# Kept weight sums, a later place for two steps of level sums, and outputs behind the next group's products in a transformer block

## The chip, the cores and the metric

The kernel runs on one core of one Trainium2 chip. The metric is the device time of one execution in microseconds. In the profile, PE is TensorE's matmul, PEld its weight load, DVE is VectorE, ACT is ScalarE, POOL is GpSimd, and SP is SyncE, which here only issues DMAs. A name with a q (SPq, POOLq, ACTq) is that engine's instruction queue.

## The reference

The input x holds 32 sequences of 64 tokens with 1024 features, in fp32. A block of four layers is computed, with one residual around the first two and one around the last two:

```python
x = x + attn(cond(x, label))        # cond: x W^T + LoRA chosen by the sequence's label
x = x + ffn(cond2(x, language))     # both: x W^T + a top-2 mixture of 8 LoRA experts of rank 16
```

The attention has 32 heads of 32 features, 8 key and value heads, rotary embedding and a causal mask. Nothing non-linear stands between cond and the projections of q, k and v, nor between cond2's base and ffn's base.

## The kernel before

**Products.** Every large product is one of 2 x 2 blocks done with seven products instead of eight (Strassen's scheme in Winograd's form). `Group` (L236) is one such product: the steps p1 to p7 each multiply one factor of the weights with one of the columns (`mult`, L268, whose matmul is L270), into three PSUM banks x, y and z. p1 goes to x and is copied to SBUF by ACT (L291); p6 goes to y and is taken out by DVE with p1 added (L297, "u1"); p5 goes to z; p7 adds to y, and is taken out (L309, "u2"); `out11` takes z out; p2 adds to x; p3 adds to z and p4 to y, and both are taken out. A bank that is accumulated on or reused has to be taken out first, so DVE's place in these steps matters to PE. The weights' factors are four sums of a weight tile, made on POOL by `weight_sums` (L171; its four additions are L180, L182, L184 and L186). The columns' sums are made on DVE by `column_sums` (L189; L195, L197, L199, L201).

**Stages.** First the weights are merged, once: cond into the projections of q, k and v (cq and ckv, `multiply` at L722 and L755, into the DRAM tensor `cqkv`), and cond2 into ffn (cf, L852, into `cf7`). Then the tokens go in two halves (`hf`, L967). In each half: six `qk_pair` products (L1025; pairs 4, 0, 1, 2, 3, 5, of which 4 are k and 5 are v), the attention in eight units, the output projection (`o_pairs`), and the feed-forward part, in 14 `quarter` groups (L1490).

**cf's levels.** In the feed-forward part each of the seven products is itself one of 2 x 2 blocks, so `cf7` holds the weights of both levels. `levels` (L823) makes them on DVE while cf's groups are multiplied: `level_one` (L803) makes sums of cf's blocks, `level_two` (L813 to L816) the four sums of one factor, and SP stores four parts of it (L818). The table `after` of L854 tells behind which step of which group (`(2, "p7")` is group 2's p7) each of them is recorded; PE, DVE and SP keep this order, as it is recorded under `tc.manual_schedule`. DVE takes cf's banks out at L603 (all blocks but the first) and adds the identity at L606. Each of these writes into a block of the tile `cf`, which is shared by groups 0 and 2 and by groups 1 and 3. `levels(0, "p6")` and `levels(0, "p7")` read the block "12" of groups 0 and 1; p4 of group 2 overwrites it. `narrow` (L769) is a small product behind some groups. `wo_sums` (L781) loads a part of the output projection's weights, makes their sums on POOL and stores them (L787) for later; its tiles have one buffer each.

**The pairs.** `qk_pair` loads a pair's merged weights w with SP, makes their sums s with POOL, in both halves, and returns a `RankGroup`. Its tiles w and s have two buffers each, so that those of one pair come free when the pair before the last is done with them. Pair 5's sums are made in two parts: the first when the pair is made (L1273), the others behind p4 of pair 3 (L1281). In the second half pair 4 is recorded to be issued behind the last sum of the first half's feed-forward part (L1166).

**The feed-forward groups.** `Quarter` (L351) splits its steps in `begin` (p1, p6), `middle` (p5, p2, p7, out11; in the last group of a half p5, p7, p2, out11) and `end` (p4, p3). The loop at L1608 records the begin of one group, the end of the one before, and the middle:

```python
group = quarter(n, r)
group.begin()
...
if last is not None:
    finish(last)
...
group.middle((n, r) == (6, 1), behind)
```

`finish` (L1553) is the end and, for the two groups of n = 4 alone, the sums that give two blocks of output: POOL adds z to b (L1560), DVE makes the output (L1562), and ACT issues its store (L1565). `known` (L1509) adds further products on POOL (L1512). PE and POOL keep the recorded order there; DVE's order is a scheduler's.

**The beginning.** DVE clears a tile (L130) and PE multiplies it (L133), ahead of the first loads' landing.

Of the kernel before, what the change touches and what calls it, by code (L numbers as in the profile page):

```python
# [13 lines left out]
F32 = mybir.dt.float32  # L14
# [5 lines left out]
P = 128  # L20
# [55 lines left out]
def block_kernel(ctx: ExitStack, tc: tile.TileContext, a, out: bass.AP):  # L76
    nc = tc.nc
# [48 lines left out]
        )  # L126
    )

    idle = tmp("idle")
    nc.vector.memset(idle, 0.0)  # L130
    ps = ps_tile("idle")
    for n in (512,):
        nc.tensor.matmul(ps[:, :n], idle[:, :P], idle[:, :n], start=True, stop=True)  # L133
    bqkv, bo, bb = biases[:, 0:12], biases[:, 12 : 12 + KC], biases[:, 12 + KC :]

# [215 lines left out]
    class Quarter(Group):  # L351
# [11 lines left out]
            self.p6()  # L363

        def middle(self, last=False, behind=None):
            two = (self.p7, self.p2) if last else (self.p2, self.p7)
            self.p5()
            if behind is not None:
                behind()
            for step in (*two, self.out11):  # L370
                step()

        def end(self):
            self.p4()
# [137 lines left out]


    cf7 = scratch.tile([P, 7, 8, 2, 2, P], F32, tag="cf7", name="cf7")
    FACTORS = ("s1", "s2", "11", "21", "12", "22", "s3", "s4")
    b1q = const.tile([P, NQ], F32, tag="b1q", name="b1q")
    b1d = const.tile([P, 6, P], F32, tag="b1d", name="b1d")
# [8 lines left out]
    with tc.tile_pool(name="gen", bufs=1) as gen:  # L526
# [320 lines left out]
        def first_w(w):  # L847
# [14 lines left out]
                (1, "p3"): lambda w: levels(0, "p3"),  # L862
                (1, "p4"): lambda w: narrow(1, w),
                (2, "p6"): lambda w: (levels(0, "p4"), wo_sums(5)),
                (2, "p7"): lambda w: (levels(0, "p6"), wo_sums(6)),
                (2, "p2"): lambda w: levels(0, "p7"),
                (2, "p3"): lambda w: wo_sums(7),
                (2, "p4"): first_w,
                (3, "out11"): lambda w: levels(1, "out11"),
                (3, "p2"): lambda w: levels(1, "p2"),  # L870
# [96 lines left out]
    for hf in range(2):  # L967
# [57 lines left out]
        def qk_pair(g, z_bank=group_bank, sums=range(4)):  # L1025
            w = first_pass.pop(f"w{g}", None)
            if w is None:
                w = load_w(cqkv[:, :, g * WG : (g + 1) * WG], f"qk{hf}{g}")

            def out(r, c, ps, add):  # L1030
                oc = 2 * g + r
                raw = tmp(f"raw_{hf}_{oc}_{c}")
                bias = bqkv[:, oc : oc + 1]
                if add is None:
                    nc.scalar.activation(raw, ps, AF.Identity, bias=bias)
                else:
                    nc.vector.scalar_tensor_tensor(raw, ps, bias, add, ALU.add, ALU.add)
                if g == 5:
                    v_blocks[r, c] = raw
                else:  # L1040
                    rope(oc, c, raw)

            def rank(r, c, rows):
                b = b1d[rows, g, :] if (r, c) == (0, 1) else b1q[rows, (2 * g + r) * P : (2 * g + r + 1) * P]
                return b, low_half(c)[rows]

            s = weight_sums(w, f"qk{hf}{g}", None, sums)
            pair = RankGroup(f"qk{hf}{g}", w, s, xt, out, rank, z_bank)
            pair.w_and_s = w, s
            return pair  # L1050
# [203 lines left out]
        with tc.manual_schedule():  # L1254

            rotated()
            pair, held = qk_pair(2), None
            for u in range(2):
                g = pair
                g.p1()  # L1260
                g.p6()
                if u == 0:
                    g.p5()
                    masked(u)
                else:
                    masked(u)
                    g.p5()
                maxima(u)
                g.p7()
                g.p2()  # L1270
                normalised(u)
                if u == 1:
                    pair = qk_pair(5, sums=(0,))  # L1273
                g.together(held)
                if u == 0:
                    pair = qk_pair(3, ps_tile)
                held = g
                g.p4()
                if u == 1:
                    w, s = pair.w_and_s  # L1280
                    weight_sums(w, None, s, (1, 2, 3))  # L1281
                g.p3()


            g, ws = pair, {}
            g.p1()
            g.p5()
            ws[0] = turned(0, in_place_of(1, "ws0"))
            g.some((0, 0), (1, 1), held=held)
            held.out01()  # L1290
            g.p6()
            prepared(2)
            ws[1] = turned(1, in_place_of(2, "ws1"))
            rotated()
            normalised(2)
            g.p7()
            g.out11()
            prepared(3)
            g.p2()
            g.out(0, 0, g.x, None)  # L1300
            g.some((1, 0), (0, 1))
            wo0 = o_load(0, 0)
            ws[2] = turned(2, in_place_of(3, "ws2"))
            normalised(3)
            g.p4()
            prepared(4)
            g.p3()
            g.out01()
            v_turned(0)
            ws[3] = turned(3, in_place_of(4, "ws3"))  # L1310
            v_turned(1)
            normalised(4)
            masked(5)
            for u in range(4):
                banks = iter((group_bank, ps_tile if u % 2 else group_bank))
                values(u, ws[u], lambda name: next(banks)(name))
                if u == 1:
                    two = [in_place_of(j, f"sums_o{j}") for j in (1, 2)]
                    t0 = [t[:, 2 * i : 2 * i + 2] for t in two for i in range(2)]
                    o_sums(0, t0, 0, 2)  # L1320
            o_sums(0, t0, 2, 4)
            maxima(5)
            wo1 = o_load(0, 1)
            ot = Columns(o_columns(0), 512, 2, [[t[:, kc, :] for kc in range(2)] for t in t0])
            pairs = o_pairs(0, 0, wo0, ot, (group_bank, group_bank))
            pairs += o_pairs(0, 1, wo1, ot, (group_bank, group_bank))
            for u in range(4, 8):
                o = pairs[u - 4]
                ws = turned(u, in_place_of(3 + u % 2, f"ws{u}"))
                o.p1()  # L1330
                if u == 7:
                    t1 = [
                        [ep.tile([P, 512], F32, tag="e", name=f"sumo{hf}{j}{kc}") for kc in range(2)]
                        for j in range(4)
                    ]
                    o_sums(1, t1, 4, 7)
                sc = scores(u + 2) if u < 6 else None
                o.p6()
                if u < 7:
                    normalised(u + 1)  # L1340
                if u < 6:
                    masked(u + 2, sc, range(2))
                o.p5()
                o.p7()
                if u < 6:
                    masked(u + 2, sc, range(2, 4))
                o.out11()
                o.p2()
                if u < 6:
                    maxima(u + 2, range(2))  # L1350
                if u == 6:
                    wo0 = o_load(1, 0)
                values(u, ws)
                o.p4()
                if u < 6:
                    maxima(u + 2, range(2, 4))
                o.p3()
            o_sums(1, t1, 7, 8)
            ot = Columns(o_columns(1), 512, 2, t1)
            wo1 = o_load(1, 1)  # L1360
            pairs = o_pairs(1, 0, wo0, ot, (group_bank, ps_tile))
            pools.close()

            yp = scoped(f"sums_y{hf}", side="right")
            xt = columns(f"y{hf}", yp, x_half, 512)
            for p in range(2):
                for step in ("p1", "p6", "p5", "p7", "p2", "out11", "p4", "p3"):
                    for o in pairs:
                        getattr(o, step)()
                    if p == 1 and step in ("p5", "out11"):  # L1370
                        xt.make(("p5", "out11").index(step))
                pairs = o_pairs(1, 1, wo1, ot, (group_bank, ps_tile))
            attention.close()
# [176 lines left out]
            group.n_q = n, q  # L1550
            return group

        def finish(group):  # L1553
            group.end()
            n, q = group.n_q
            if SEVEN[n][0] == "p5":
                for m in range(2):
# [9 lines left out]
        with tc.manual_schedule(engines={mybir.EngineType.PE, mybir.EngineType.Pool}):  # L1567
# [40 lines left out]
            for n in range(7):  # L1608
# [10 lines left out]
                for r in range(2):  # L1619
# [5 lines left out]
                    if r == 0 and n < 6:  # L1625
                        differences_of[n + 1] = experts_difference(n + 1)
                    if last is not None:
                        finish(last)
                    behind = {(0, 0): next_logits, (0, 1): next_turned}.get((n, r))
                    group.middle((n, r) == (6, 1), behind)  # L1630
                    if (n, r) == (0, 1):
                        hw[1] = scaled("3", hf, [h[1, c] for c in range(2)], late["gs"])
                        through.update({"21": hw[1][0], "22": hw[1][1]})
                        nc.vector.tensor_sub(et[:, 1], hw[1][1], et[:, 0])
                        nc.vector.tensor_sub(hw[0][1], hw[1][1], hw[0][1])
                    if r == 0 and n < 6:
                        ts[n + 1] = inner_columns(n + 1)
                    last = group
            finish(last)
        pools.close()  # L1640


# [86 lines left out]
```

## Time and profile before

| | us |
|---|---|
| Median of 3 runs | 1195.55 |
| The three runs | 1189.01, 1195.59, 1195.55 |
| The profiled execution | 1194.38 |
| Its span, first to last instruction | 1192.6 |
| PE busy | 1176.1 |
| DVE, POOL, ACT busy | 707.1, 551.0, 163.8 |

The profile is of one execution. Its own time is 1.8 us longer than its span, and 1.2 us shorter than the median of the runs. Positions in time are given from the start of the span: the weights are merged until about 299 us, the first half of the tokens goes from there to about 740 us, and the second to the end. A matmul in fp32 shows as two instructions, and its end is modelled, so that a group of eight instructions of 512 columns is printed as 3.60 us while the next follows after 3.43. The granted clock of TensorE is 1 at full speed.

### The profile page before, as it was taken

How to read it: one execution, taken by the hardware profiler on the slowest of the kernel's cores; microseconds unless marked ns; L12 is line 12 of the kernel's file. 1: busy time of each engine (PE TensorE's matmuls, PEld its weight loads, DVE VectorE, ACT ScalarE, POOL GpSimd, SP SyncE). 2: the span in 40 equal slices, each digit the busy share in tenths (PEclk: the TensorE clock that was granted, in tenths of full speed). 3: DMA queues.
4: the chain of work that ended last, by engine and by line, in shares of the span. 5: the costliest groups of instructions: out<-in, count | busy, mean ns of one | idle time of the engine just before them, and what ended most of it. 6: DMA issues, size and time to landing. Idle time of an engine off the chain costs nothing.

```text
span 1192.6 us, 14868 instructions
## 1 busy us (share of the span) xinstructions
PE 1176.1 (99%) x5752; PEld 673.4 (56%) x5752; DVE 707.1 (59%) x1215; ACT 163.8 (14%) x314; POOL 551.0 (46%) x491
## 2 busy tenths in 40 slices
PE   9999999989999999999999999999999999999998
PEld 3444874545444446544458888444446544448887
DVE  3214162638555878874647664756788874657563
ACT  1100000000000115430011000100114530011000
POOL 1452355360343667662703654344677661801342
PEclk9999999999999999999999999999999999999999
DMA  9553644867311122022315668111121022203544
GB/s 318 169 212 127 265 147 142 276 210 253 92 35 36 36 72 71 2 71 71 103 32 164 185 184 259 36 39 35 37 70 50 24 71 71 93 16 102 154 144 139
DMA packets 120373, 137.60 MB, mean 115 GB/s; under 512 B 6768, under 2 KB 98928, under 8 KB 119024
## 3 DMA queue, kind: packets, MB, share of 16 engines
q1 hardware_dynamic: 105312, 111.65, 30.0%
q10 hardware_dynamic: 12304, 16.62, 4.0%
q0 software_dynamic: 2688, 8.39, 2.0%
q8 instruction: 45, 0.74, 0.3%
q14 instruction: 24, 0.20, 0.1%
HBM read 101.94 MB, written 34.71 MB: 115 GB/s over the span
## 4 chain that ended last, share of the span: by engine, by line
PE 93%; DVE 5%; issue 1%; DMA 1%; SPq 0%; ACT 0%
PE qk_y L270 10%; PE o_y L270 7%; PE qk_z L270 7%; PE qk_x L270 7%; PE f_y L270 6%; PE o_z L270 5%; PE o_x L270 5%; PE f_z L270 4%; PE f_x L270 4%; PE cq_y L270 4%; PE sc L1078 3%; PE cf_y L270 3%; PE cq_x L270 3%; PE pt L1137 2%; PE cq_z L270 2%; PE cf_z L270 2%
## 5 line engine op out<-in xcount | busy, mean ns | idle before, releaser
L1013 POOL TENSOR_TENSOR raw<-raw,consts 128x512 f32<-128x512 f32 x40 | 62.8, 1579 | 105.2 <-DVE t L1012 105.2
L270 PE MATMUL qk_y<-sum_x,s_qk 128*128 128x512 f32 x192 | 87.7, 597 | 2.3 <-DVE sum_x L197 2.1
L1111 POOL TENSOR_TENSOR e<-e,top 128x512 f32<-128x512 f32 x64 | 66.3, 1054 | 48.5 <-DVE top L1110 46.9
L270 PE MATMUL qk_x<-x,w_qk 128*128 128x512 f32 x192 | 86.8, 595 | 0.0
L270 PE MATMUL f_y<-s_f,w_f 128*128 128x256 f32 x336 | 82.8, 380 | 2.1 <-DVE f_u L309 2.1
L1129 POOL TENSOR_TENSOR e<-e,tot 128x512 f32<-128x512 f32 x64 | 64.8, 1045 | 28.7 <-DVE tot L1127 27.3
L270 PEld LDWEIGHTS f_y<-s_f,w_f 128*128 128x128 f32 x336 | 63.6, 190 | 11.9 <-DVE f_u L309 3.4
L270 PEld LDWEIGHTS qk_y<-sum_x,s_qk 128*128 128x128 f32 x192 | 35.6, 190 | 48.0 <-issue 40.7
L270 PEld LDWEIGHTS qk_x<-x,w_qk 128*128 128x128 f32 x192 | 36.1, 190 | 45.3 <-issue 45.0
L270 PE MATMUL o_x<-q,w_o 128*128 128x512 f32 x128 | 58.9, 592 | 0.0
L1248 POOL TENSOR_TENSOR x<-x,o_u 128x512 f32<-128x512 f32 x24 | 30.9, 1291 | 54.5 <-DVE o_u L1246 33.2
L1014 DVE TENSOR_TENSOR t<-t,consts 128x512 f32<-128x512 f32 x40 | 49.7, 1253 | 0.7
L1101 DVE TENSOR_TENSOR e<-sc,consts 128x512 f32<-128x512 f32 x64 | 41.2, 677 | 11.0 <-PE sc L1078 11.0
L1121 ACT ACTIVATE e<-e 128x512 f32<-128x512 f32 x64 | 37.9, 639 | 58.9 <-POOL e L1111 58.8
L1126 DVE TENSOR_REDUCE tot<-e 128x8 f32<-128x512 f32 x64 | 40.3, 666 | 7.4 <-ACT e L1121 7.3
L934 POOL COPY gatesr<-oh1r 128x1024 f32<-128x1024 f32 x4 | 4.1, 1037 | 86.8 <-DVE oh1r L932 86.8
L270 PE MATMUL qk_y<-sum_x,w_qk 128*128 128x512 f32 x96 | 44.2, 603 | 0.0
L270 PE MATMUL qk_z<-x,s_qk 128*128 128x512 f32 x96 | 43.4, 594 | 0.0
L270 PE MATMUL qk_z<-sum_x,s_qk 128*128 128x512 f32 x96 | 43.4, 594 | 0.0
L1110 DVE TENSOR_REDUCE top<-e 128x8 f32<-128x512 f32 x64 | 41.3, 679 | 0.8
L1023 DVE TENSOR_TENSOR q<-raw,t 128x512 f32<-128x512 f32 x32 | 38.5, 1204 | 2.5 <-POOL raw L1013 2.3
L1139 ACT COPY ws<-pt 128x512 f32<-128x512 f32 x64 | 33.4, 608 | 40.7 <-PE pt L1137 40.7
(382 smaller groups left out, 2363.9 us busy)
## 6 DMA issues: line engine op xcount, KB each, us to landing
w_f<-cf SPq DMA_DIRECT2D x28, 512.0 KB, 4.6
w_qk<-cqkv SPq DMA_DIRECT2D x12, 1024.0 KB, 5.5
w_f<-cf SPq DMA_DIRECT2D x28, 384.0 KB, 4.7
x<-in_xT SPq DMA_DIRECT2D x16, 512.0 KB, 6.4
w_o<-in_wo SPq DMA_DIRECT2D x16, 512.0 KB, 4.4
s_o<-wos SPq DMA_DIRECT2D x16, 512.0 KB, 6.3
outT<-o ACTq DMA_DIRECT2D x20, 256.0 KB, 4.2
cqkv<-cq ACTq DMA_DIRECT2D x16, 256.0 KB, 5.3
```

Of the source, the lines that this page charges most:

```text
L270: self.last = nc.tensor.matmul(ps, self.weights[left][:, kc, :], self.right(right, kc), start=first and kc == 0, stop=kc == self.h - 1, sk ...
L1013: nc.gpsimd.tensor_mul(rv, rv, c3)
L1014: nc.vector.tensor_mul(t2v, t2v, s3)
L1023: nc.vector.tensor_add(*unfinished.pop())
L1078: nc.tensor.matmul(sc[j][:, n * S : (n + 1) * S], q[rows, g, b, 2 * mp : 2 * mp + 2, :].rearrange("p m t -> p (m t)"), k[rows, g, b, :], s ...
L1101: nc.vector.tensor_add(per_key(e), per_key(sc[j]), mask.unsqueeze(1).to_broadcast([P, 8, S]))
L1110: nc.vector.tensor_reduce(top, ev, AX.X, ALU.max)
L1111: nc.gpsimd.tensor_sub(ev, ev, wide(top))
L1121: nc.scalar.activation(e, e, AF.Exp, scale=SCALE)
L1126: nc.vector.tensor_reduce(tot[:, i], es[i], AX.X, ALU.add)
L1129: nc.gpsimd.tensor_mul(es[i], es[i], wide(tot[:, i]))
L1139: nc.scalar.copy(ws, pt)
```

## The change

Four things are changed.

1. `qk_pair` makes the sums s in the first half only. It stores them in a new DRAM tensor `sqk` with a DMA of 1 MB issued by POOL (pair 5's after its second part). In the second half s is loaded from there, by SP, and for pair 4 by POOL.
2. In cf's table, `levels(0, "p6")` moves from behind p7 of group 2 to behind its out11, and `levels(0, "p7")` from behind its p2 to behind its p3, ahead of `wo_sums(7)`. `wo_sums(6)` stays behind p7, so that its load is now ahead of the stores of levels p6 on SP.
3. What `finish` did after the end of a group is now `sums_out`, recorded behind the next group's middle. In the last group of a half, p7 is now ahead of p5.
4. The first tile is cleared in 256 columns, and multiplied three times.

```diff
-    idle = tmp("idle")
+    idle = tmp("idle")[:, :256]
...
-    for n in (512,):
+    for n in (256, 256, 256):
         nc.tensor.matmul(ps[:, :n], idle[:, :P], idle[:, :n], start=True, stop=True)
...
         def middle(self, last=False, behind=None):
-            two = (self.p7, self.p2) if last else (self.p2, self.p7)
+            if last:
+                self.p7()
             self.p5()
             if behind is not None:
                 behind()
-            for step in (*two, self.out11):
-                step()
+            self.p2()
+            if not last:
+                self.p7()
+            self.out11()
...
+    sqk = scratch.tile([P, 6, 4, H, P], F32, tag="sqk", name="sqk")
...
                 (2, "p6"): lambda w: (levels(0, "p4"), wo_sums(5)),
-                (2, "p7"): lambda w: (levels(0, "p6"), wo_sums(6)),
-                (2, "p2"): lambda w: levels(0, "p7"),
-                (2, "p3"): lambda w: wo_sums(7),
+                (2, "p7"): lambda w: wo_sums(6),
+                (2, "out11"): lambda w: levels(0, "p6"),
+                (2, "p3"): lambda w: (levels(0, "p7"), wo_sums(7)),
...
-            s = weight_sums(w, f"qk{hf}{g}", None, sums)
+            if hf == 0:
+                s = weight_sums(w, f"qk{hf}{g}", None, sums)
+                if len(sums) == 4:
+                    nc.gpsimd.dma_start(sqk[:, g], s)
+            else:
+                s = wp.tile([P, 4, H, P], F32, tag="s", name=f"s_qk{hf}{g}")
+                (nc.gpsimd if g == 4 else nc.sync).dma_start(s, sqk[:, g])
...
-                if u == 1:
+                if (u, hf) == (1, 0):
                     w, s = pair.w_and_s
                     weight_sums(w, None, s, (1, 2, 3))
+                    nc.gpsimd.dma_start(sqk[:, 5], s)
...
-        def finish(group):
-            group.end()
+        def sums_out(group):
             n, q = group.n_q
             if SEVEN[n][0] == "p5":
...
                     if last is not None:
-                        finish(last)
+                        last.end()
                     behind = {(0, 0): next_logits, (0, 1): next_turned}.get((n, r))
                     group.middle((n, r) == (6, 1), behind)
+                    if last is not None:
+                        sums_out(last)
...
-            finish(last)
+            last.end()
```

## The prediction

> **What bounds the kernel now.** I read the page's busy shares first, then the waits of PE (TensorE matmul), then the timelines around each.
>
> ```profile
> PE 1176.1 (99%) x5752; PEld 673.4 (56%) x5752; DVE 707.1 (59%) x1215; ACT 163.8 (14%) x314; POOL 551.0 (46%) x491
> ```
>
> PE is busy 1176.1 of 1192.6 us, so no change that leaves its products alone can win more than about 16 us plus what its matmuls lose to a lower clock or to restarts. PE's waits (who waited for whom: total us, times, longest) are few:
>
> ```profile
> PE cf_z L270 <- DVE cf L603: 4.4, 1, 4.4
> PE f_y L270 <- DVE f_u L309: 2.1, 3, 0.9
> PE qk_y L270 <- DVE sum_x L197: 2.1, 4, 0.5
> PE idle L133 <- DVE idle L130: 1.5, 1, 1.5
> PE av L1152 <- ACT q L1160: 1.3, 1, 1.3
> ```
>
> The change touches the first four. POOL's 551 us bound nothing by themselves; they count only where they slow DVE or hold PE.
>
> **Part 1: cf's levels.** PE's timeline (start, us, what, idle before and its releaser):
>
> ```profile
> 237.46 3.60 PE L270 MATMUL cf_x<-w,w_cf 128*128 128x512 f32 x8
> 245.50 5.09 PE L270 MATMUL cf_z<-w,s_cf 128*128 128x512 f32 x8 [4.44 <-DVE cf L603]
> 250.43 3.60 PE L270 MATMUL cf_y<-sum_cf,w_cf 128*128 128x512 f32 x8
> ```
>
> and DVE's in the same stretch:
>
> ```profile
> 237.66 0.69 DVE L309 TENSOR_TENSOR cf_u<-cf_y,cf_p 128x512 f32<-128x512 f32 x1 [3.33 <-PE cf_y L270]
> 238.27 2.49 DVE L803 TENSOR_TENSOR cfs<-cf,cfs 128x512 f32<-128x512 f32 x2
> ...
> 244.68 0.68 DVE L603 TENSOR_TENSOR cf<-cf_z,cf_u 128x512 f32<-128x512 f32 x1
> ```
>
> L603 empties bank z, which p3's product needs. It stands behind the six operations of levels p6 (238.27 to 244.68). Moved ahead of them it starts at 238.35 and ends at 239.1; p2's product ends at about 241.06 (245.50 - 4.44), so p3 starts with no wait. Between 241.06 and the next step (250.43) lie 9.37 us where four undisturbed products take 3.43 (the spacing of such groups): 5.94 us, of which 4.44 are the wait and 1.50 the slower matmuls after it (5.09 against 3.60).
>
> Those 1.50 are a clock matter: the granted clock is 0.50 from 245.0 to 248.4, and PE had been busy 0.06 us of the 4.0 us before. [...] As the sum is made against this execution, I start from the row.
>
> Against that stands a wait that comes nearer. With its loads, wo_sums(6) is now ahead of levels p6's four stores on SP, and its load waits for POOL's sums, which end at 245.3 (POOL's L186). So those stores, issued from 243.1 before, start at about 245.8, and the stores of block 12 after them are issued until about 250.6 (249.6 before). DVE's L603 of p4 overwrites that block and must wait for them: they land at about 254 (252.9 before, when its wait ended, plus one). It empties bank y, which group 3's p6 needs at 241.06 + 3.43 (p3) + 3.43 (p4) + 3.71 (narrow) + 3.43 (p1) = 255.06, where it was 261.0. L603 takes 0.69, so the slack falls from 6 us to about 0.4. Cost: 0 to 1.5 us; I take 0.4, as the later stores only move by about one us. **Part 1: 5.5 us saved (4.4 to 5.9).**
>
> **Part 2: the sums' outputs.** In each half, before the p4 of group (5,0):
>
> ```profile
> 710.96 3.43 DVE L1562 SCALAR_TENSOR_TENSOR o<-z_f,consts,a_f 128x512 f32<-128x512 f32 x2
> ```
>
> holds back L309 (714.71), for which PE waits 0.91 us. Start to start, the last matmul of p6 and the first of p4 lie 1.29 us apart, not 0.22, and the four behind the wait take 1.13, not 1.03: 1.17 us, twice: 2.35. Moved behind middle(), L309 can follow p7's product at once. Late next are what now follows the two L1562 (3.4 us, from about 714.3): L297 of group (5,1), which ends near 718.1 and frees the bank that p7 needs at about 719.3, and the stores on ACT, behind which the next p1's copy stands, not needed for 5 us. Slack 1.2 us. **2.3 us saved (1.2 to 2.4).**
>
> **Part 3: the kept sums of q, k and v.** In the second half 24 POOL sums (1.26 to 1.76 us each, about 37 us) go. PE does not wait for them; their worth is at the opening of that half. DVE's column sums run there beside POOL's sums (740.1 to 753.6), and PE waits for each:
>
> ```profile
> 745.71 6.79 DVE L197 TENSOR_TENSOR sum_x<-x,sum_x 128x512 f32<-128x512 f32 x4
> ```
>
> The same four in the first half, with POOL still:
>
> ```profile
> 294.62 2.49 DVE L197 TENSOR_TENSOR sum_x<-x,sum_x 128x512 f32<-128x512 f32 x4
> ```
>
> Without POOL's sums L195 and L197 end at 740.1 + 2 x 2.45 = 745.0, before p6 can start (745.12 + 1.92 = 747.04). p6 ended at 753.51 instead of 750.5, and the wait for L297 behind it (0.21, with restarts 0.45) goes too: 3.45 us to win.
>
> The price is the loads. s_qk14 is issued on POOL behind the last sum. The last group's p7 is moved ahead of p5 (1.3 us), so that sum ends at about 735.7, not 737.0; the issue costs 0.56 (row L787). It must land by 747. w_qk14, issued at 733.19, takes 6.8 us: it lands at 740.0, and PE needs it at 741.49. But the DMA engines are full there (second last number: their busy share; last: GB/s):
>
> ```profile
> 736.00:738.00 2.00, 2.00 (x11) 1.75 (x10) 1.09 (x3) 0.00 (x0) 0.72 (x1) 1.00 0.92 298
> ```
>
> By the row alone, a 1 MB load of 5.5 to 7 us lands by 743.5, and everything is won: 3.45. [...] I take 2.2, between, since the first packets of a POOL issue come late (POOL's own stores of 0.5 MB take 5.5 us to land).
>
> All else lies beside PE's work. SP: s_qk10 waits for the half's last product, and w_qk10 behind it, needed 31 us later; the other four are issued with their w, 25 us ahead of use (w_qk issues at 770.93, 796.24, 821.54, 850.22), for 5.5 us of transfer. First half: six 1 MB stores on POOL, each 0.30 + 0.56 us of its queue (row L787), once ahead of a rope product (409.52, then 442.85) whose sums DVE adds one block later: hidden, 0.9 us each if not. I put 0.3 for them. **Part 3: 1.9 us saved (-0.5 to 3.4).**
>
> **Part 4: idle.** The memset halves (0.48 to about 0.25), and the 512 columns (2.08 us) become 768 (about 2.9): PE works from about 1.25 to 4.17 instead of 1.47 to 3.55, and the first real product waits for its load until 4.29 anyway. PE then runs 5 matmuls in the 3.4 us before 9.4 and 7 in the 2.6 after it: full speed from 9.4. A window earlier would save 3.4 / 2 = 1.7 us; no effect, 0. The phase decides; I take 0.6.
>
> **Sum.** 5.5 + 2.3 + 1.9 + 0.6 = 10.3 us. The profiled execution took 1194.38 (span 1192.6 and 1.8 around it), 1.2 less than the median of 1195.55; the runs lie between 1189.01 and 1195.59. 1194.38 - 10.3 = **1184.1 us**, 0.96% under the median. About 1% is what a measurement of this kernel can tell from no change; the border is 1183.6.
>
> **Rivals.**
> - *The opening becomes a DMA wait* (0.15): w_qk14 late by 2 to 4 us; Part 3 is worth -0.5 and the time 1186.5. For it: the 0.92. Against it: POOL issues late, when most of w_qk14 is through.
> - *cf's wait moves to bank y* (0.10): the stores of block 12 land 4 us later than I count, and Part 1 keeps only 1.5: 1188.1. For it: 2.5 MB in about 8 us, at a time that runs at 273 to 377 GB/s.
> - *All upper ends* (0.10): 5.9 + 2.4 + 3.4 + 1.7 - 0.3 = 13.1, 1181.3.
> - *Slower* (0.04): the five loads of s on SP come late for their p6. They have 25 us; to eat the 10.3 us won, each must be 2 us late, that is land 27 us after issue where a w_qk takes 5.5; to be slower by 1% (1207.5), each 4.7 us late. Nothing in the trace suggests it.
> - *The sums' removal does nothing*, PE being full: that is so for 20 of the 24, and counted.
>
> **Chances.** The likeliest case has 0.61, alone 1181.5 to 1187. The range to 8 in 10 is 1181 to 1188.5: it takes in the first three rivals. Faster by over 1% are the upper ends and half of the likeliest case: 0.40. Within 1%: 0.57. Slower: 0.03.
>
> **What would show it.** p3's cf_z starts within 0.3 us of p2's end, and no granted clock under 1 near 245; the f_y waits of 0.9 are gone, only the first (0.3) left; L197 of the second half near 2.5 us for four; waits for DMA at qk_x or qk_y near 741 to 750 tell the rival, as does cf_y waiting on L603 near 255. Wrong I am if PE's busy share falls, or a new wait of PE over 2 us stands in the list.

## The result, and the profile after

| | before | after |
|---|---|---|
| Median, run side by side (us) | 1194.8 (4 runs, 1189.01 to 1195.59) | 1182.77 (4 runs, 1182.09 to 1183.37) |
| Ratio, 95% interval | | 0.9909 (0.9881 to 0.9936) |
| The profiled execution, its span | 1194.38, 1192.6 | 1182.32, 1180.3 |

By the ratio the kernel is faster by 0.9%, and the medians lie 12.0 us apart; the forecast was 1184.1 (1181.0 to 1188.5). The interval holds the border of 1%, so the gain is not told apart from one of just over or just under that.

From the page after, the busy shares:

```profile
PE 1171.8 (99%) x5756; PEld 673.8 (57%) x5756; DVE 697.9 (59%) x1215; ACT 163.9 (14%) x314; POOL 519.1 (44%) x474
```

PE's waits after (who waited for whom: total us, times, longest):

```profile
PE av L1163 <- issue: 1.4, 1, 1.4
PE idle L133 <- DVE idle L130: 1.2, 1, 1.2
PE cq_x L270 <- DMA w_cq<-in_w: 0.6, 2, 0.5
PE pt L1148 <- DVE e L1112: 0.4, 2, 0.3
PE pt L1148 <- ACT ws L1150: 0.4, 2, 0.3
PE f_y L270 <- DVE f_u L309: 0.3, 1, 0.3
PE h L481 <- issue: 0.3, 1, 0.3
```

The waits of 4.4, of 0.9 twice and of 2.1 at qk_y are gone. The one at the attention's values (av) has stayed, and a small new one stands at the product h; both are now put down to "issue", that is, to nothing that the profile shows. More of these two below.

**cf's levels.** PE's timeline after:

```profile
235.96 3.60 PE L270 MATMUL cf_x<-w,w_cf 128*128 128x512 f32 x8
239.40 3.60 PE L270 MATMUL cf_z<-w,s_cf 128*128 128x512 f32 x8
242.83 3.60 PE L270 MATMUL cf_y<-sum_cf,w_cf 128*128 128x512 f32 x8
```

p3's cf_z follows p2's cf_x after 3.44 us, with no wait and at full clock. DVE's timeline in the same stretch says why, and answers the fear about bank y:

```profile
236.16 0.69 DVE L309 TENSOR_TENSOR cf_u<-cf_y,cf_p 128x512 f32<-128x512 f32 x1 [3.33 <-PE cf_y L270]
236.89 0.69 DVE L607 TENSOR_TENSOR cf<-cf_z,cf_u 128x512 f32<-128x512 f32 x1
...
253.05 0.69 DVE L607 TENSOR_TENSOR cf<-cf_y,cf_p 128x512 f32<-128x512 f32 x1 [7.28 <-DMA cf<-cf]
```

L607 (L603 of before) now comes right behind L309. The p4 of group 2 did wait for the stores of block 12, until 253.05, as I had said; but group 3's p6 had started at 253.40, before this taking-out ended (253.74), so in another bank. There are three such banks (`group_bank`), and p1 and p6 of group 3 had two, so that the one of p4 was left for its p5, at 256.84: 3.1 us of slack, not 0.4.

**The outputs, the opening and the first tile.** In the kernel after, L309 goes ahead of the two outputs (L1574, L1562 of before), and L197 of the second half takes as long as in the first:

```profile
705.16 0.42 DVE L309 TENSOR_TENSOR f_u<-f_y,f_p 128x256 f32<-128x256 f32 x1 [0.31 <-PE f_y L270]
706.83 3.02 DVE L1574 SCALAR_TENSOR_TENSOR o<-z_f,consts,a_f 128x512 f32<-128x512 f32 x2
...
733.86 2.49 DVE L197 TENSOR_TENSOR sum_x<-x,sum_x 128x512 f32<-128x512 f32 x4
```

PE runs from p6 to p4 (f_y, eight instructions in one go), and through p6 of pair 4 (qk_y), without a wait:

```profile
705.82 1.89 PE L270 MATMUL f_y<-s_f,w_f 128*128 128x256 f32 x8
738.92 3.70 PE L270 MATMUL qk_y<-sum_x,s_qk 128*128 128x512 f32 x8
```

The products of the first tile, before and after:

```profile
1.47 2.08 PE L133 MATMUL idle<-idle 128*128 128x512 f32 x2 [1.47 <-DVE idle L130]
```

```profile
1.20 2.93 PE L133 MATMUL idle<-idle 128*128 128x256 f32 x6 [1.20 <-DVE idle L130]
```

**Where 12.3 us of span come from.** The same matmul can be looked up in both traces (the ones of idle left out), and the difference of its two start times read along the program. The steps of that difference:

| Place | predicted | before to after, these two traces |
|---|---|---|
| Start, part 4 | 0.6 | 1.5 (1.2 by the 17th matmul of cq, 0.3 at 66 us) |
| cf, part 1 | 5.5 | 6.1 |
| Sums' outputs, part 2 | 2.3 | 2.4 (1.2 and 1.2) |
| Opening of the second half, part 3 | 1.9 | 2.9 (3.4 won, 0.5 lost at h) |
| Elsewhere | 0 | -0.3 (0.2 lost at 596 us, 0.1 at 897 us) |
| Sum | 10.3 | 12.6 at the last matmul, 12.3 of span |

### The profile page after: what moved, and what is told of

Same layout as the page of the kernel before. It is cut to its first block, busy times and chain, and to the rows that moved or that the text cites. A ratio compares the mean times of both kernels' runs of the same rounds, so it can differ in the third digit from the quotient of the medians.

```text
span 1180.3 us, 14885 instructions
## 1 busy us (share of the span) xinstructions
PE 1171.8 (99%) x5756; PEld 673.8 (57%) x5756; DVE 697.9 (59%) x1215; ACT 163.9 (14%) x314; POOL 519.1 (44%) x474
## 4 chain that ended last, share of the span: by engine, by line
PE 98%; DVE 1%; DMA 1%; issue 0%; SPq 0%; ACT 0%
PE qk_y L270 11%; PE o_y L270 7%; PE qk_x L270 7%; PE qk_z L270 7%; PE f_y L270 6%; PE o_z L270 5%; PE o_x L270 5%; PE f_z L270 4%; PE f_x L270 4%; PE cq_y L270 4%; PE cf_y L270 3%; PE sc L1089 3%; PE pt L1148 2%; PE cf_x L270 2%; PE cq_z L270 2%; PE cf_z L270 2%
## 5 line engine op out<-in xcount | busy, mean ns | idle before, releaser
L1112 DVE TENSOR_TENSOR e<-sc,consts 128x512 f32<-128x512 f32 x64 | 41.1, 676 | 10.3 <-PE sc L1089 10.3
```

Source lines behind the costliest of these rows:

```text
L1112: nc.vector.tensor_add(per_key(e), per_key(sc[j]), mask.unsqueeze(1).to_broadcast([P, 8, S]))
```

## The experiments

Each ran in several executions beside the kernel before (56 runs of it with the first four experiments, 11 with the next four, 27 with the last four). What I give as "by the trace" is the difference in start times as above.

### One part at a time

`e_cf` is the kernel before with the three lines of cf's table changed, and nothing else:

```diff
-                (2, "p7"): lambda w: (levels(0, "p6"), wo_sums(6)),
-                (2, "p2"): lambda w: levels(0, "p7"),
-                (2, "p3"): lambda w: wo_sums(7),
+                (2, "p7"): lambda w: wo_sums(6),
+                (2, "out11"): lambda w: levels(0, "p6"),
+                (2, "p3"): lambda w: (levels(0, "p7"), wo_sums(7)),
```

> The kernel before with cf's table alone changed. Theory (the positions of PE's matmuls in the two profiles): 6.0 us less (4.4 of wait and 1.5 of slower matmuls), p3's cf_z right behind p2's cf_x, no wait at cf_y. [...] Rival 2 (the wait moves to bank y, by the later stores of block 12): a new wait at group 3's p6 and only 1.5 to 4 less.

Measured: 1187.93 (1186.9 to 1189.5, 11 runs), ratio 0.9966 (0.9950 to 0.9982); by the trace 6.1 at cf against the profile of before. No wait at cf_y. But the means of the runs lie only 4.5 apart (1192.42 and 1187.94). The 56 runs of before show the reason: they are two groups. 24 lie between 1188.5 and 1191.3, 32 between 1192.0 and 1198.3, and the profile that I had read was one of the upper. With `e_cf` all eleven lie within 2.6 us. What differs between the groups is seen in the next three.

`e_out` is the kernel before with point 3 of the change (`sums_out` and `middle`) alone:

```diff
...
-                        finish(last)
+                        last.end()
...
+                    if last is not None:
+                        sums_out(last)
```

> The kernel before with the sums' outputs behind the next group's products, and the last group's p7 ahead of p5, alone. Theory: 2.3 us less (1.1 and 1.2 in the two halves). Rival (the outputs hold the next group instead): 0 to 1 less, with a new wait at f_y or f_x. [...]

Measured: 1191.1 (22 runs), ratio 0.9986 (0.9972 to 1.0000); by the trace 1.2 and 1.2 at the two f_y, where the waits of 0.9 are gone and no new one has come.

`e_sqk` is the kernel before with the kept sums alone:

```diff
-            s = weight_sums(w, f"qk{hf}{g}", None, sums)
+            if hf == 0:
+                s = weight_sums(w, f"qk{hf}{g}", None, sums)
+                if len(sums) == 4:
+                    nc.gpsimd.dma_start(sqk[:, g], s)
+            else:
+                s = wp.tile([P, 4, H, P], F32, tag="s", name=f"s_qk{hf}{g}")
+                (nc.gpsimd if g == 4 else nc.sync).dma_start(s, sqk[:, g])
...
```

> The kernel before with the kept sums of q, k and v alone. Theory: 2.8 us less, all at the opening of the second half (3.3 won, 0.3 to 0.5 lost again to a short wait there), and nothing in the other five pairs, PE being full. Rival 1: the gain at the opening came from the last group's earlier p7 (not in this kernel), and 1 or less is left. Rival 2: the loads cost as much as the sums, 0.

Measured: 1192.37 (14 runs), ratio 0.9994 (0.9976 to 1.0011), too wide to tell the theory from nothing; by the trace 2.5 at the opening (3.4 won, 0.8 lost at h), and nothing at the five other pairs.

`e_idle` is the kernel before with 256 columns cleared and three products of them:

```diff
-    idle = tmp("idle")
+    idle = tmp("idle")[:, :256]
...
-    for n in (512,):
+    for n in (256, 256, 256):
```

> The kernel before with the first tile's change alone. Theory: PE's full clock starts some 3 to 5 us earlier, at about 4 to 6 instead of 9.4, and 1.5 us are won (0 to 1.7 by the phase). Rival: the earlier clock of the profile after was chance of the phase, and nothing is won (within 0.5). The wait in the attention's values of the second half, 1.3 long, comes at the 62nd of its matmul instructions as in the kernel after, not at the 66th as before, if it belongs to a place in PE's instructions: this kernel has four instructions more ahead of it.

Measured: 1193.35 (22 runs), ratio 1.0004 (0.9990 to 1.0018); by the trace 1.5 at 68 us. The times do not show it, the traces of all experiments together do. Those with the old first tile (before, `e_cf`, `e_out`, `e_sqk` and a later one) start the 17th matmul of cq at 13.2 to 14.5, mean 13.98; the nine with the new tile at 12.3 to 12.7, mean 12.51. The ranges do not touch: 1.47 us, and at the 981st matmul, ahead of cf's wait, still 1.40. The full clock, by its record in each trace, starts at 8.0 to 10.7 with the old tile (9.4 in before, where cq's matmuls follow one another after 0.85 us ahead of it and 0.43 behind it), and at 4.0 to 7.3 with the new (4.0 in after). What is won at the start can be lost again: in one of the nine (`e_after_again`) PE, being early, waited at 67 us for POOL's sums of cq, and of 1.3 us only 0.2 were left at 90 us:

```profile
67.17 3.70 PE L270 MATMUL cq_y<-sum_cq,s_cq 128*128 128x512 f32 x8 [0.94 <-POOL s_cq L182]
```

**Why before has two groups.** PE's line of p3 in `e_out`, and the same in `e_sqk`, both with cf's table as before:

```profile
245.10 5.37 PE L270 MATMUL cf_z<-w,s_cf 128*128 128x512 f32 x8 [3.36 <-DVE cf L606]
```

```profile
243.26 3.67 PE L270 MATMUL cf_z<-w,s_cf 128*128 128x512 f32 x8 [1.45 <-DVE cf L604]
```

The wait was 4.44 in the profile of before, 3.36 in `e_out`, 1.45 in `e_sqk` and 0.98 in `e_idle`. In front of p3's taking-out stand the six operations of levels p6; in `e_sqk` they are

```profile
239.65 1.28 DVE L804 TENSOR_TENSOR cfs<-cf,cfs 128x512 f32<-128x512 f32 x2
240.96 0.43 DVE L814 TENSOR_TENSOR cft0s<-cfs,cfs 128x256 f32<-128x256 f32 x1
241.42 0.43 DVE L815 TENSOR_TENSOR cft0s<-cft0s,cfs 128x256 f32<-128x256 f32 x1
241.76 0.42 DVE L816 TENSOR_TENSOR cft0s<-cfs 128x256 f32<-128x256 f32 x1
242.10 0.42 DVE L817 TENSOR_TENSOR cft0s<-cfs,cft0s 128x256 f32<-128x256 f32 x1
```

2.9 us in all, with POOL doing nothing between 238.8 and 244.2. In the profile of before the same six took 6.4, beside POOL's sums of cf's last group and of the output projection, which ran from 236.0 to 245.3 without a pause of note. So the length of the wait goes with the place where POOL's sums happen to fall. And where it was long, the clock fell: after the waits of 4.44 and 3.36 it was 0.50 for 3.4 us, after those of 1.45 and 0.98 it stayed full.

I tried to fix the place of POOL's sums. `e_cf_wload` is the kernel before with the load of cf's last group moved to another queue:

```diff
...
-                    ws.append(load_w(a[inner][which[len(ws)]], f"{name}{len(ws)}"))
+                    ws.append(load_w(..., nc.gpsimd if (name, len(ws)) == ("cf", 3) else nc.sync))
```

> The kernel before, with one thing changed: the weights of cf's last group (1 MB) are loaded by POOL's queue instead of SP's, where they stand behind five stores of levels. Theory (the runs of the kernel before fall into two groups, near 1189.6 and near 1194.5, and what decides is when that load lands: late, POOL's sums of it run beside the six DVE operations of levels p6, which take 6.4 us instead of 3.3 to 4, and PE's wait is 3.4 to 4.4 with a clock drop instead of 1 to 1.5 without): the load lands early in every run, the wait at cf_z is 1 to 1.5, and all runs lie at 1188 to 1191. Rival (the two groups have another cause): runs at 1193 and above stay.

Measured: 1191.58 (1188.61 to 1194.43, 22 runs) beside 1194.38; ratio 0.9985 (0.9973 to 0.9998). The theory as I put it failed: the runs over 1193 are fewer (4 of 22, against 18 of 27 of the kernel before), not gone, and its profile has the wait:

```profile
244.53 5.37 PE L270 MATMUL cf_z<-w,s_cf 128*128 128x512 f32 x8 [3.35 <-DVE cf L603]
```

POOL's own line tells that the load, issued at 224.33 there, came hardly earlier:

```profile
224.33 0.53 POOL L445 DMA_DIRECT2D w_cf<-in_w  x1 [1.48 <-PE cx L773]
234.54 1.26 POOL L180 TENSOR_TENSOR s_cf<-w_cf 128x512 f32<-128x512 f32 x1 [9.68 <-DMA w_cf<-in_w]
```

Ten microseconds for 1 MB, beside the stores of the levels. And the sums of the output projection that follow (from 240.95) slowed three of the six operations again. That POOL's work beside the six makes the wait fits all five traces; what decides in a given execution where it falls, beyond the landing of that load, stays open.

### Which sums paid at the opening

`e_pair4_sums` is the kernel after, with pair 4's sums made again:

```diff
-            if hf == 0:
+            if hf == 0 or g == 4:
...
```

> The kernel after, but the sums of pair 4 are made by POOL again in the second half; the other five pairs load theirs. Theory (only pair 4's sums matter, PE being full over the other twenty): the gain at the opening of the second half is gone, 2.5 to 3.3 us longer than the kernel after, waits for DVE sum_x and qk_u at qk_y as before. Rival (the five later loads, or the sums of POOL in the whole half, carry a part): clearly less than 2 longer.

Measured: 1183.63 (5 runs; ratio 0.9917, 0.9901 to 0.9933), within 1 of the kernel after. My theory fell. `e_sums_and_load` keeps the load, and lets POOL add for nothing beside it (an output nobody reads):

```diff
+                if g == 4:
+                    spare = tmp("spare").rearrange("p (k o) -> p k o", o=P)
...
+                    nc.gpsimd.tensor_add(spare, a21, a22)
+                    nc.gpsimd.tensor_sub(spare, spare, a11)
+                    nc.gpsimd.tensor_sub(spare, a11, a21)
+                    nc.gpsimd.tensor_sub(spare, a12, spare)
```

> The kernel after, with the load of pair 4's sums kept, and four POOL additions of the same size added behind it, into a tile that nobody reads. Theory (POOL's additions beside DVE's column sums slow DVE, from 2.5 to 6.8 us for four, and PE waits for those): DVE's L197 is slow again and some 2 to 3 us of the opening's gain are lost though s is loaded. Rival (what counts is that s itself comes early): no longer than the kernel after by more than 0.5.

Measured: 1183.43 (5 runs; ratio 0.9916). DVE in `e_pair4_sums` (the other has the same, 4.63 and 4.65):

```profile
731.11 4.63 DVE L195 TENSOR_TENSOR sum_x<-x 128x512 f32<-128x512 f32 x4
735.66 4.64 DVE L197 TENSOR_TENSOR sum_x<-x,sum_x 128x512 f32<-128x512 f32 x4
740.22 2.48 DVE L199 TENSOR_TENSOR sum_x<-x,x 128x512 f32<-128x512 f32 x4
```

DVE is slowed as I said, and PE's p6 still doesn't wait: POOL is done at 738.5, the last of L197's four columns is there at 740.3, and p6, which starts at 739.77, takes it 2.6 us after its start (four times two instructions, each time 0.86). Even without the wait of 1.5 at h in front of it p6 would have come to it at 740.9. In `e_sums_and_load`, where the wait at h is 0.6, the same sum gives 741.6 against 741.1. In the kernel before, L195 and L197 took 12.5 us (5.71 and 6.79), and POOL went on with the sums of pair 0 after 0.35 us. Hence `e_both_sums`, the kernel after with the sums of both:

```diff
-            if hf == 0:
+            if hf == 0 or g in (4, 0):
...
```

> The kernel after, with the sums of the pairs 4 and 0 made by POOL again in the second half; four pairs load theirs. Theory (it is pair 0's sums, which followed pair 4's on POOL, that slowed DVE's column sums at the time when PE waited for them): 1.5 to 3 us of the opening's gain are lost, with waits at qk_y for sum_x or qk_u. Rival (DVE's delay does not reach PE in the changed kernel, as with pair 4's sums alone): within 1 of the kernel after.

Measured: 1185.66 (6 runs; ratio 0.9940, 0.9918 to 0.9963) beside 1183.21 for the kernel after on that chip: 2.5 lost, as the theory had it. DVE's timeline, and PE's:

```profile
741.16 5.70 DVE L199 TENSOR_TENSOR sum_x<-x,x 128x512 f32<-128x512 f32 x4
```

```profile
749.93 3.70 PE L270 MATMUL qk_y<-sum_x,s_qk 128*128 128x512 f32 x8 [2.35 <-DVE qk_u L297]
```

Pair 0's sums run from 738.88 to 745.72 there. They slow L199 (5.70 instead of 2.48), L297 stands behind it on DVE, and PE waits for L297. In the kernel before, the wait was one step earlier, for L197. So of the 24 sums taken away, pair 4's alone cost nothing, pair 0's four on top of them cost the time, and the other sixteen show no step in the trace of `e_sqk`. Pair 0's alone were not tried, so that the cost may need both.

### The two waits for "issue"

`e_s14_sp` is the kernel after, with all of s loaded by SP:

```diff
-                (nc.gpsimd if g == 4 else nc.sync).dma_start(s, sqk[:, g])
+                nc.sync.dma_start(s, sqk[:, g])
```

> The kernel after with pair 4's s loaded by SP right behind its w instead of by POOL. Theory A (the wait of 0.3 at the product h, to 0.7 in the kernel with the kept sums alone, is for s's landing): s lands earlier, the wait goes, 0.3 less. Theory B (the wait is for PE's next page of instructions, a load of 16 KB on an own queue, kept back by the two 1 MB loads): s lands earlier, and the wait stays where it is in PE's instructions as long as the loads run when the page is asked for; 0 to 0.3 less. Either way the time is within 0.5 of the kernel after.

Measured: 1184.46 (6 runs; ratio 0.9926, 0.9911 to 0.9941). The wait at h stayed (0.7, until 738.07), though s was issued at 715, and even w, issued 9 us behind it in the same queue, landed at 733.1: theory A is out. A new wait of 0.5 came, for w_qk at qk_x: in one queue s goes ahead of w, and w took 9.0 us to land instead of 7.0. It was 1.3 to 1.7 above the two medians of the kernel after, more than I had expected of either theory.

Theory B counts instructions. Counting PE's matmuls, weight loads and semaphore instructions in the trace of the kernel after, the wait at h stands ahead of record 7105 and the one at the values ahead of 9153: 2048 lie between. In `e_idle` and after, with eight records more at the start than before, the values' wait comes at the 62nd of its matmul instructions, in before and `e_cf` at the 66th (four of the eight are matmuls, the others weight loads):

```profile
922.48 2.32 PE L1152 MATMUL av<-ws,v 64*32 64x256 f32 x66 [1.53 <-issue]
```

is the line of `e_idle` (66 of 128 are left), and that of `e_cf` is

```profile
921.61 1.96 PE L1152 MATMUL av<-ws,v 64*32 64x256 f32 x62 [0.87 <-ACT q L1160]
```

with ACT named though its place, not ACT, is what moved. The page's queue table has a queue for this:

```profile
q8 instruction: 45, 0.74, 0.3%
```

45 packets of 16 KB. That each of them is a block of PE's instructions is my reading, from the queue's name. The count fits: in the kernel after the 45 packets landed on average 255 of PE's records apart, and the 2048 between the two waits are 8 times 256. I counted a boundary every 256 records, back and forth from those two. At 43 of the boundaries the landing was 2.0 us or more ahead of the first record behind the boundary in the kernel after, and the list of waits has nothing there; at h and at the values it was 1.5 and 1.3 us ahead, and PE stood. In all the traces PE stood 20 times at these two places (by 0.2 to 1.8 us), and each time went on 1.3 to 1.5 us after a packet had landed. The DMA view of after for 911.8 to 914.8 shows only data, and for 914.8 to 917.4 the block:

```profile
q1 hardware_dynamic: 254, 0.93, 85.9%
```

```profile
q8 instruction: 1, 0.02, 2.3%
q1 hardware_dynamic: 9, 0.02, 2.0%
```

`e_later_load` holds back one data load, that of s of the second output group:

```diff
-            wo0 = o_load(0, 0)
+            wo0 = o_load(0, 0, (0,))
...
             normalised(4)
+            o_load(0, 0, (1,), wo0)
```

> The kernel after, with one of the output projection's loads (s of its second group, 0.5 MB, needed some 14 us later) issued behind the exponentials' sums of unit 4 instead of ahead of them; one DVE clearing of a column holds it back. Theory (the wait of 1.4 in the attention's values is for a page of PE's instructions, which lands only when the data loads of 909 to 914 end): the page lands earlier and 0.5 to 1.4 us of the wait go. Rival (the wait is ACT's copies, or bound to the place itself): the wait stays at 1.3 to 1.5.

Measured: 1183.12 (5 runs; ratio 0.9912, 0.9896 to 0.9928). The block landed at 913.7 instead of 916.1, and the wait of 1.4 is off the list; by the trace 1.8 were won there, and 1.1 of them given back by 935, by the values' matmuls, which followed one another more slowly, there and in their next place at 931. `e_pages` holds back pair 0's two loads as well, by an ACT copy of one column that the loads must follow:

```diff
+            if (hf, g) == (1, 0):
+                w = wp.tile([P, KC, WG], F32, tag="w", name=f"w_qk{hf}{g}")
+                nc.scalar.copy(w[:, 0, :1], late["first"].add10[:, :1])
+                nc.sync.dma_start(w, cqkv[:, :, g * WG : (g + 1) * WG])
...
+                if g == 0:
+                    nc.scalar.copy(s[:, 0, 0, :1], late["first"].add10[:, :1])
```

> The kernel after, with the later load of the second output group as before, and pair 0's two loads of the second half (1 MB each, needed 30 us later) held back until the first copy of pair 4's p1, some 6 us later. Theory (a page of PE's instructions, asked for near 731, lands late because these loads keep the DMA engines busy): the wait of 0.3 to 0.7 at the product h goes, and the 1.4 at the values too; 0.5 to 1.5 less than the kernel after. Rival: the wait at h stays, since w and x of that time fill the engines until 735 anyway.

Measured: 1181.96 (1181.32 to 1183.46, 6 runs), ratio 0.9911 (0.9889 to 0.9932). PE's waits in it:

```profile
PE idle L133 <- DVE idle L130: 1.2, 1, 1.2
PE pt L1154 <- DVE e L1118: 0.4, 2, 0.3
PE pt L1154 <- ACT ws L1156: 0.4, 2, 0.3
PE f_y L270 <- DVE f_u L309: 0.3, 1, 0.3
PE cq_x L270 <- DMA w_cq<-in_w: 0.2, 1, 0.2
```

Both waits are gone. `e_after_again` is the kernel after once more, beside it:

> The kernel after once more, beside the others on the same chip: 1182 to 1184, in one group, since its wait at cf_z is gone.

Measured: 1183.21 (1182.28 to 1183.42, 6 runs; ratio 0.9917, 0.9895 to 0.9938), one group as expected. The means of `e_pages` and of this are 1182.14 and 1183.05: 0.9 less, the best of all that ran, by less than a measurement here can settle.

## Why the prediction was right, point by point

**Part 1** was right in kind, and 0.6 short: the row (4.44 + 1.50) held whole. It was even 0.16 too small, since I counted from the modelled end of p2 (241.06) and not from 237.46 + 3.43, where the next product can start. The 0.4 that I took off for bank y was owed to a wrong idea of which bank comes next. The clock: three profiles had a wait of 3.35 to 4.44 there, and in each the granted clock dropped to 0.50 for 3.4 us. So the row held: a wait of this length cost 1.5 to 1.8 more (5.09 and 5.37 against 3.60). In `e_out` and `e_cf_wload` the drop began 1.1 and 1.2 us after PE had gone on, so that of the 3.4 us ahead of it PE had been idle only 2.2 to 2.3. From which length of a wait on the clock drops was not shown: after the 1.45 of `e_sqk`, and after the 2.35 at qk_y in `e_both_sums` (mean granted clock 1.000), it stayed full.

What the prediction missed is that this row was one of two kinds. It was worth 6.1 against the profiled execution, but about 1.7 against the lower group of before. With the runs split by whether their mean granted clock is 1.000, before has medians of 1189.59 (22 runs) and 1194.49 (34, two of the low ones among them); `e_out` 1186.84 and 1191.65, `e_sqk` 1188.06 and 1193.09, `e_idle` 1188.95 and 1193.78. Within a group, then, the outputs are worth 2.8, the kept sums 1.4 to 1.5, and the first tile 0.6 to 0.7; with 1.7 for cf they make 6.6, and 1189.59 - 6.6 = 1183.0 is the kernel after. So the change is worth about 6.6 us (0.6%) against the lower group, and 11.5 against the upper; that three of the four executions of before in the result were of the upper is chance, and with it nearly half of the 12.0. By the traces the kept sums and the first tile were worth about one more each than these medians show (2.5 and 1.5). The wait at 67 us in `e_after_again` is one place where such a gain is lost again; the rest of the difference stays open. The range of 1189.01 to 1195.59 in the three runs of before was the hint that I noted and did not follow.

**Part 2**: 2.3 predicted, 2.4 measured. The two things named as late next took nothing.

**Part 3**: the 3.45 to win were 3.4. The term that was mis-sized is the price of the loads, 1.3 in my sum and 0.5 in fact. The rival (w_qk14 starved by s_qk14) did not come: w_qk14 took 7.0 us to land instead of 6.8, and s_qk14, which I had at 5.5 to 7, took 9.9, beside two more loads of 1 MB that SP issued from 729.3 on. No run shows the 2.2 of my sum, nor the w_qk14 late by 2 to 4 of the rival, which were my estimates; in their place the two traces show 3.4 won and 0.5 lost at h. The row alone was right for w. But the two loads hardly met: issued at 727.05, s_qk14 moved its first packet at 730.3, and w_qk14 landed at 731.6. POOL's packets came late, as I had said, and by then w_qk14 was nearly through. In one queue, ahead of w, s did make it late (`e_s14_sp`, 0.5). The 0.5 lost at h I had not foreseen; it is the late block of instructions.

**Part 4**: 0.6 predicted out of 0 to 1.7, 1.5 measured in the mean of nine profiles against five. I took a third of the upper end because I did not know when the full clock would begin; the nine began it at 4.0 to 7.3, never as late as the earliest of the old, 8.0. What I called a window can be read off the two traces: the granted clock stayed the same for 235.52, 3.413 and 945.49 us in before (full, 0.50, full) and for 1177.60 in after (full), which is 69, 1, 277 and 345 times 3.413. The phase is where the first of these begins, 9.4 in before and 4.0 in after.

**The rivals.** "All upper ends", 1181.3 at 0.10, was nearest to the median of 1182.77: Parts 1, 2 and 4 ended at or near their upper ends. "Slower" had nothing: the five loads by SP were never waited for. That twenty of the 24 sums cost nothing holds, but those of the pair that is multiplied there cost nothing alone; pair 0's on top of them did.

## What to carry to other kernels

A wait that one profile shows at one length may have another in the next execution: when the runs of the kernel before spread by more than the change is worth, find the wait that varies before pricing its removal from one row. When two engines share work at a place where PE waits, ask what else follows in the other engine's queue, since here the harm came only when the next group's sums followed. And when a wait for "issue" keeps its place in an engine's instruction count, while everything around it moves, look at the packets of the queue "instruction": here PE went on 1.3 to 1.5 us after one had landed, and did not stand where the data loads in front of that packet were held back.

## What was not expected of the hardware

- At two places of its instruction stream, the same in kernel after kernel, PE stood still for 0.2 to 1.8 us, until 1.3 to 1.5 us after a packet of the queue "instruction" had landed. In the kernel after these landed at 735.8, amid data packets, and at 916.1, when the data loads had just ended (the last packet at 915.2). Where the loads were moved out of the way (`e_pages`), PE did not stand.
- DVE's subtractions of 256 columns took 0.42 alone, and 0.83 to 1.48 beside POOL's sums; those of 512 columns 0.62 (2.49 for four), and up to 1.7 (6.79 for four).
- A load of 1 MB issued by POOL moved its first packet only 3.3 us after its issue, and took 9.9 us; the load of SP ahead of it took 7.0, against 6.8 without it.
